# Text by image tokens as 77 extra columns of the first layer's v products

## The chip, the cores and the metric

The kernel runs on one core of a Trainium2 chip. The metric is the device time of one execution in microseconds; the median of three runs stands for a kernel. All arrays are fp32. TensorE is the matrix engine, DVE (VectorE), ACT (ScalarE) and POOL (GpSimd) are the engines for elementwise work, SP issues most of the loads.

## The reference

Two layers of cross attention from 100 queries to 722 context tokens (77 of text, 645 of image), for a batch of 8, with 640 channels in 20 heads and a context width of 1024. Both layers read the same context, with weights of their own. What bears on the change is the second layer's extra term `sem`: it needs the product of every text token with every image token of the same batch entry.

```python
# both layers: attention over the text tokens plus attention over the image tokens
text = ctx_2048[:, :77]                    # B, 77, 1024
ip   = ctx_2048[:, 77:]                    # B, 645, 1024
q = x @ Wq;  k_text = text @ Wk;  v_text = text @ Wv     # first layer: W.T
ip_k = ip @ Wk_ip;  ip_v = ip @ Wv_ip
...
# second layer only
text_probs = softmax((q @ k_text^T) * scale)             # B, 100, 77, over all 640 channels
q_sem = text_probs @ text                                # B, 100, 1024
sem   = (q_sem @ ip^T) * scale                           # B, 100, 645
fused = scores_ip + 0.5 * sem                            # the same sem for all heads
ip_probs = softmax(fused) * spatial_mask
...
out = (text_out + ip_out) @ Wout + bout + residual
```

The kernel forms `sem` as `text_probs @ (text @ ip^T)`. The inner product `text @ ip^T`, 77x645 for each batch entry and independent of the layer, is what the change makes in another place.

## The kernel before

A *unit* u is one layer of one batch entry: units 0 to 7 are the first layer, 8 to 15 the second. There are three kinds of work.

**The prologue** (some 205 us) makes the first layer's q and both layers' k and v of the text tokens, `text_k` and `text_v`/`text_v_blocks`, and in `left_v` the v rows of the last 5 of the 645 image tokens, all stored to DRAM.

**Projection of the image tokens.** Units 0 to 13 are taken in pairs of batch entries (`pair_tasks`). A pair runs over five blocks j of 128 image tokens (the last block has 133 for k, 128 for v). `load_x` brings the tokens of both entries, x with 1024 features on partitions in eight chunks. A pair and its block form a 2x2 product of halves (entry by half of the features, times half of the features by half of the channels), done with seven products in place of eight: `token_sums` makes four sums of x (DVE, POOL), `weight_sums` four sums of the weights, and `seven` runs the products named first, sixth, second, seventh, fifth, fourth, third, with PSUM tiles a to e (second adds onto a, third onto d). In `v_product` the tokens are the stationary operand and 320 weight columns stream through, four matmuls a product (line 482); in `k_product` the weights are stationary (line 490); `last_k` makes the last 128 channels of k plainly (line 461). ACT and DVE bring the results from PSUM to `vo` and `ko`, and POOL stores them to DRAM. The weights lie in quarters `wv00`, `wv01`, `wv10`, `wv11` (first digit the half of features, second the half of channels) and sums `wvt2` to `wvt4`. Unit 14 (`single_tasks`) and unit 15 (`last_tasks`) are made with plain products (`plain_product`, line 558).

The second layer's pairs also have `text_by_image`: for each of the two entries and each block, eight matmuls with 77 text columns stationary and the block's image tokens streaming (line 472, PSUM tile `psg`), an ACT copy to `gst` (line 477) and a POOL store to `g_d` (line 478). For units 14 and 15 `text_one` does the same in blocks of 256, 256 and 133 tokens. The text is loaded as `textt`.

**Attention.** Each unit has five phases p of four heads each, 80 phases in all: `scores` (in two parts), softmax on DVE and ACT, `transposes` of the probabilities (PSUM `pspt`, line 857), `values` (PSUM `pv`, line 879). For the second layer, `small_work` puts `sem_logits`, `sem_transpose` and `sem_scores` into phases 3 and 4 of the unit before; `sem_scores` multiplies the 100x77 probabilities with the loaded `g` (77x645), which `load_g` fetches from `g_d` in phase 4.

TensorE's order is written by hand. `production` spreads the projection's tasks over the phases in front of their need (`spread`, by planned times such as 2.15 for a v step), and the main loop puts them between the pieces of attention, so that TensorE has a product to do while DVE and ACT work on the softmax. The first pair is made before phase 0. PSUM has four banks for scores, two for `ps_pt` (transposes, values, small work) and two for the projection's products (`ps_pj`). The order of the other engines follows from the program and its dependences.

Of the kernel before, what the change touches and what calls it, by code (L numbers as in the profile page):

```python
# [14 lines left out]
P = 128  # L15
B = 8
# [27 lines left out]
def two_layer_xattn(  # L44
# [36 lines left out]
    g_d = [dram.tile([NT, NI], F32, tag=f"g_{b}", name=f"g_d{b}") for b in range(B)]  # L81
# [16 lines left out]

    def load_quarter(kind, rows, n, i, j):
        t = wpool.tile([P, HK, n], F32, tag=f"w{kind}{i}{j}", name=f"w{kind}{i}{j}")  # L100
        nc.sync.dma_start(t, rows[:, HK * i : HK * (i + 1), n * j : n * (j + 1)])
        W[kind, f"b{i + 1}{j + 1}"] = t

    def weight_sums(kind, n, engines):
        b11, b12, b21, b22 = (W[kind, f"b{x}"] for x in ("11", "12", "21", "22"))
        t2, t3, t4 = (wpool.tile([P, HK, n], F32, tag=f"w{kind}t{x}", name=f"w{kind}t{x}") for x in (2, 3, 4))
# [29 lines left out]
    def seven(name, product, area):  # L136

        c11, c12, c21, c22 = area
# [17 lines left out]
        def second():  # L156
            product(ps["a"], 2, True)
            nc.scalar.copy(c11, flat("a"))

# [5 lines left out]
        def fifth():  # L165
            ps["d"] = product_ps(f"{name}_d")
            product(ps["d"], 5, False)
            nc.vector.tensor_tensor(c22, flat("d"), c21, ALU.add)

        def fourth():  # L170
            ps["e"] = product_ps(f"{name}_e")
            product(ps["e"], 4, False)
            nc.vector.tensor_tensor(c21, flat("e"), c21, ALU.add)  # L173

# [5 lines left out]

    WHICH = {1: "b11", 2: "b21", 3: "b22", 4: "t4", 5: "t1", 6: "t2", 7: "t3"}
# [11 lines left out]
    with ExitStack() as es:  # L193
# [101 lines left out]
        def text_v_blocks(l):  # L295
            for r in range(2):
# [38 lines left out]

        def sums_of(kind):
            weight_sums(kind, {"v": HC, "k": 2 * P}[kind], (nc.vector, nc.gpsimd))

        with tc.manual_schedule(engines={mybir.EngineType.PE}):
# [11 lines left out]
            left_v(0)  # L351
            text_v(1)
            sums_of("v")
            load_left(1)
            text_v_blocks(1)
            sums_of("k")
            left_v(1)

# [50 lines left out]
    def load_g(u):  # L409
        t = one.tile([NT, NI], F32, tag="g", name=f"g_{u}")  # L410
        nc.sync.dma_start(t, g_d[u % B])
# [15 lines left out]
    def pair_tasks(us):  # L427
# [3 lines left out]
        if l:  # L431
            text = {}

            def load_text():
                text[0] = one.tile([P, NCC, 2 * NT], F32, tag="textt", name=f"textt_{us[0]}")
                b = us[0] % B
                nc.sync.dma_start(text[0], text_t.rearrange("k p n -> p k n")[:, :, b * NT : (b + 2) * NT])

            tasks.append((0.0, load_text))
        for j, (n0, n1) in enumerate(BLOCKS):  # L440
            n = n1 - n0
            sums, vo, ko = {}, {}, {}
# [26 lines left out]
            def text_by_image(i, j=j, n0=n0, n=n):  # L469
                ps = product_ps(f"psg_{us[i]}_{j}")  # L470
                for k in range(NCC):
                    nc.tensor.matmul(
                        ps[:NT, :n], lhsT=text[0][:, k, i * NT : (i + 1) * NT], rhs=xs[j][:, i, k, :n],
                        start=(k == 0), stop=(k == NCC - 1),
                    )
                t = one.tile([NT, NX], F32, tag="gst", name=f"gst_{us[i]}_{j}", bufs=2)
                nc.scalar.copy(t[:, :n], ps[:NT, :n])  # L477
                nc.gpsimd.dma_start(g_d[us[i] % B][:, n0 : n0 + n], t[:, :n])

            def v_product(ps, which, go_on, sums=sums):  # L480
                for k in range(HK):
                    nc.tensor.matmul(  # L482
                        ps[:, :HC], lhsT=sums[which][:, k, :P], rhs=W["v", WHICH[which]][:, k, :],
# [12 lines left out]
            def v_step(i, j=j, vo=vo, made={}, v_product=v_product):  # L496
                if i == 0:
                    o = vo[0]
                    made[j] = seven(
                        f"psv_{us[0]}_{j}", v_product, (o[:, 0, :HC], o[:, 0, HC:], o[:, 1, :HC], o[:, 1, HC:])  # L500
# [20 lines left out]
            if l:  # L521
                tasks += [(1.8, lambda i=i, f=text_by_image: f(i)) for i in range(2)]
            steps = [
                [(2.15, lambda i=i, f=v_step: f(i)) for i in range(7)],
# [583 lines left out]
```

## Time and profile before

| | |
|---|---|
| median of three runs | 2108.51 us (2107.51 to 2110.2) |
| the profiled execution | 2109.68 us |
| its span, from the first to the last instruction | 2107.6 us |
| granted TensorE clock | 1.0 |
| TensorE busy | 2084.8 us, 99% |
| DVE, ACT, POOL busy | 935.6, 861.5, 331.9 us |
| PSUM tiles of text by image (`psg`) | 30 in pairs, 6 in single units |
| attention's phases | from 381 us to the end; the second layer's units are attended from 1292 us |

In the profile a row of a group gives busy time, the mean length of one instruction in ns, and the idle time of its engine before it with what ended it. In a timeline a row gives start and length in us, engine, line, and how many instructions were merged. PE rows are matmuls, PEld rows weight loads that overlap them. One fp32 matmul of the program appears as two records, a transpose as one.

### The profile page before, as it was taken

What the parts mean: (1) busy time and instruction counts of PE and PEld (TensorE: products, weight loads), DVE (VectorE), ACT (ScalarE), POOL (GpSimd) and SP (SyncE); (2) the same over time, 40 slices, a digit from 0 to 9 for tenths busy, and PEclk for the clock granted to TensorE, in tenths of its full rate; (3) what the DMA queues carried; (4) which work ended last, traced back from release to release, by engine and by line L of the source; (5) the groups of instructions that cost most, each with busy time, mean ns of one, the idle gap of its engine ahead of it and who ended that gap; (6) DMA issues with size and microseconds to landing.
All of it is one profiled execution on the core that took longest, in us unless ns stands there. A gap on an engine that the chain in (4) does not pass through costs nothing. (4 is left out here: it accounts for less than half of the span.)

```text
span 2107.6 us, 41702 instructions
## 1 busy us (share of the span) xinstructions
PE 2084.8 (99%) x16770; PEld 1691.3 (80%) x16770; DVE 935.6 (44%) x2380; ACT 861.5 (41%) x2861; POOL 331.9 (16%) x382
## 2 busy tenths in 40 slices
PE   8999999999999999999999999999999999999999
PEld 8676888787788887877888888888888788777888
DVE  2211122455444455454544454454445445555554
ACT  1001000345444444354434444444445445566665
POOL 3313111111010111111511111011111110111110
PEclk9999999999999999999999999999999999999999
DMA  9344223224235343535434343343334254434320
GB/s 347 106 135 158 92 79 103 86 79 127 73 113 145 95 106 94 157 93 153 121 119 124 91 113 98 114 119 102 95 104 117 85 146 143 135 93 132 109 82 7
DMA packets 264623, 242.00 MB, mean 115 GB/s; under 512 B 31242, under 2 KB 233178, under 8 KB 264430
## 3 DMA queue, kind: packets, MB, share of 16 engines
q1 hardware_dynamic: 245310, 171.97, 29.3%
q0 software_dynamic: 19120, 67.37, 9.5%
q8 instruction: 132, 2.16, 0.4%
q14 instruction: 61, 0.50, 0.1%
HBM read 171.68 MB, written 67.61 MB: 114 GB/s over the span
## 5 line engine op out<-in xcount | busy, mean ns | idle before, releaser
L864 DVE COPY pt<-pspt 128x400 f32<-128x400 f32 x320 | 175.8, 568 | 188.6 <-PE pspt L857 167.1
L818 ACT ACTIVATE p<-p,st 100x512 f32<-100x512 f32 (+1 forms) x320 | 176.4, 553 | 142.2 <-DVE st L814 142.2
L818 ACT ACTIVATE p<-sc,st 100x512 f32<-100x512 f32 (+1 forms) x320 | 165.0, 529 | 138.2 <-DVE st L807 138.1
L841 ACT ACTIVATE p<-p,st 100x512 f32<-100x512 f32 x320 | 204.8, 711 | 40.5 <-DVE st L837 39.4
L857 PE MATMUL pspt<-ident,p 100*128 100x100 f32 (+1 forms) x1920 | 209.9, 250 | 5.7 <-DVE res L732 4.3
L857 PEld LDWEIGHTS pspt<-ident,p 100*128 100x128 f32 (+1 forms) x1920 | 187.5, 137 | 32.7 <-DVE res L732 7.4
L862 ACT COPY pt<-pspt 128x400 f32<-128x400 f32 (+1 forms) x160 | 78.0, 488 | 232.1 <-PE pspt L857 231.2
L482 PE MATMUL psv_a<-wv,x 128*128 128x320 f32 x560 | 164.3, 436 | 1.4 <-ACT gst L477 1.2
L482 PE MATMUL psv_d<-wv,s 128*128 128x320 f32 x560 | 164.1, 436 | 0.0
L814 DVE CUSTOM_DVE_ANT_0 p<-sc,sem 100x512 f32<-100x512 f32 (+1 forms) x320 | 138.8, 490 | 29.9 <-PE sc L801 29.8
L505 POOL DMA_DIRECT2D v_d<-vo x70 | 39.1, 558 | 666.5 <-DVE vo L173 551.8
L490 PEld LDWEIGHTS psk_a<-x,wk 128*128 128x128 f32 x1120 | 133.0, 191 | 10.1 <-DVE hs L883 3.1
L482 PEld LDWEIGHTS psv_a<-wv,x 128*128 128x128 f32 x560 | 103.1, 190 | 47.4 <-issue 7.3
L482 PEld LDWEIGHTS psv_d<-wv,s 128*128 128x128 f32 x560 | 103.9, 190 | 45.4 <-issue 3.2
L490 PE MATMUL psk_d<-s,wk 128*128 128x128 f32 (+1 forms) x1120 | 139.9, 278 | 0.0
L801 PE MATMUL sc<-k,q 32*100 32x210 f32 (+1 forms) x1280 | 138.5, 502 | 0.3 <-ACT p L826 0.3
L490 PE MATMUL psk_a<-x,wk 128*128 128x128 f32 (+1 forms) x1120 | 138.4, 276 | 0.2 <-ACT ko L149 0.2
L490 PEld LDWEIGHTS psk_d<-s,wk 128*128 128x128 f32 x1120 | 131.1, 191 | 8.2 <-issue 3.5
L807 DVE TENSOR_REDUCE st<-sc 100x4 f32<-100x2048 f32 x80 | 120.1, 1501 | 31.2 <-PE sc L801 31.2
L461 PE MATMUL psk<-x,wk 128*128 128x256 f32 (+1 forms) x560 | 131.2, 383 | 1.0 <-ACT vl L333 1.0
L517 POOL DMA_DIRECT2D k_d<-ko x70 | 58.1, 830 | 463.2 <-DVE ko L173 420.3
L461 PEld LDWEIGHTS psk<-x,wk 128*128 128x128 f32 x560 | 102.2, 188 | 24.4 <-issue 7.1
(176 smaller groups left out, 3399.7 us busy)
## 6 DMA issues: line engine op xcount, KB each, us to landing
x<-ip_t SPq DMA_DIRECT2D x56, 512.0 KB
k<-k_d SPq DMA_DIRECT2D x78, 322.5 KB
v<-v_d SPq DMA_DIRECT2D x78, 320.0 KB
v_d<-vo POOLq DMA_DIRECT2D x70, 320.0 KB, 2.5
k_d<-ko POOLq DMA_DIRECT2D x56, 320.0 KB, 6.7
o<-wo SPq DMA_DIRECT2D x40, 320.0 KB
x<-ip_t SPq DMA_DIRECT2D x16, 532.0 KB
q<-wq SPq DMA_DIRECT2D x20, 320.0 KB
```

The source lines that it names most:

```text
L461: nc.tensor.matmul(ps[:, : 2 * n], lhsT=W["k", 4][:, k, :], rhs=xs[j][:, :, k, :n], start=(k == 0), stop=(k == NCC - 1),)
L482: nc.tensor.matmul(ps[:, :HC], lhsT=sums[which][:, k, :P], rhs=W["v", WHICH[which]][:, k, :], start=(k == 0 and not go_on), stop=(k == HK ...
L490: nc.tensor.matmul(ps[:, r * n : (r + 1) * n], lhsT=W["k", WHICH[which]][:, k, r * P : (r + 1) * P], rhs=sums[which][:, k, :], start=(r == ...
L517: nc.gpsimd.dma_start(k_d[u][:, :, n0 : n0 + n], ko[0][:, h, :, :n])
L801: nc.tensor.matmul(sc[:S, i, : k1 - k0], lhsT=qs_[u][rows, c, :], rhs=ks[u, c][rows, k0:k1], start=True, stop=True)
L807: nc.vector.tensor_reduce(st[:, part, :], sc[:S, :, :n], AX.X, ALU.max, negate=True)
L814: nc.vector.tensor_tensor_reduce(out=img, in0=sc[:S, i, :n], in1=sems[u][:, k0 : k0 + n], scale=-1.0, scalar=3.0e38, op0=ALU.add, op1=ALU. ...
L818: nc.scalar.activation(p[:, i, k0 : k0 + n], img, AF.Exp, bias=st[:, part, i : i + 1], scale=sign, accum_out=st[:, 3 + part, i : i + 1],)
L841: nc.scalar.activation(p[:, i, :KA], p[:, i, :KA], AF.Copy, scale=mul[:, 0, i : i + 1])
L857: nc.tensor.transpose(ps[:rows, i * S : (i + 1) * S], pr[u, c][:, i, j * P : j * P + rows], ident[:S, :S])
L862: nc.scalar.copy(dst, src)
L864: nc.vector.tensor_copy(dst, src)
```

## The change

The products of text and image tokens are no longer made in the second layer. In the first layer, four of the seven v products of a block (first, second, fifth, fourth) get 77 more columns: behind the 320 weight columns of `wv00`, `wv10`, `wv01` and `wvt4` lie text columns of the two entries. First and second give text times image for the first entry, summed in PSUM tile a. For the second entry, fifth multiplies the sum of its token halves with the first half of the text, and fourth the second token half with the difference of the text halves (`text_sum`, on POOL). `text_of` copies the columns out (ACT for the first entry, DVE for the second) and stores both with one DMA a block. The result lies in DRAM with image tokens as rows, `g_d[pair][entry, 645, 77]`. `load_text` loads the text columns for each pair, in front of the pair before's last k products. The 5 image tokens beyond 640, which the v products do not hold, are made in the prologue by `left_text` (64 small matmuls); `load_left(1)` moves ahead, and the second half of `text_v_blocks(1)` moves behind `left_v(1)`. In the second layer, `load_g` loads the rows in phase 2 of the unit before instead of phase 4, and `sem_text` turns them into the old `g` (77x645) with six transposes on TensorE and two ACT copies in phase 3. `textt`, `text_by_image` and `text_one` go.

```diff
-    g_d = [dram.tile([NT, NI], F32, tag=f"g_{b}", name=f"g_d{b}") for b in range(B)]
+    g_d = [dram.tile([2, NI, NT], F32, tag=f"g_{g}", name=f"g_d{g}") for g in range(B // 2)]
...
+    WITH_TEXT = ("wv00", "wv01", "wv10", "wvt4")
+    wide = {}
+    def weight_tile(tag, n, name=None):
+        w = HC + NT if tag in WITH_TEXT else n
+        wide[tag] = wpool.tile([P, HK, w], F32, tag=tag, name=name or tag)
+        return wide[tag][:, :, :n]
...
+    def load_text(us):
+        for i, (tag, h) in zip((0, 0, 1, 1), (("wv00", 0), ("wv10", 1), ("wv01", 0), ("wvt4", 1))):
+            b = us[i] % B
+            nc.sync.dma_start(
+                wide[tag][:, :, HC:],
+                text_t[HK * h : HK * (h + 1)].rearrange("k p n -> p k n")[:, :, b * NT : (b + 1) * NT],
+            )
+    def text_sum():
+        t = wide["wvt4"][:, :, HC:]
+        nc.gpsimd.tensor_tensor(t, t, wide["wv01"][:, :, HC:], ALU.subtract)
...
+            beside(2, ps["a"])
...
+            beside(5, ps["d"])
...
+            beside(4, ps["e"])
...
+    TEXT_AT = {1: "wv00", 2: "wv10", 5: "wv01", 4: "wvt4"}
...
+        def left_text():
+            t = fp.tile([P, 2, NT], F32, tag="evg", name="gl", bufs=1)
+            ps = product_ps("psgl")
+            for h in range(2):
+                for k in range(NCC):
+                    for i in range(4):
+                        b = 4 * h + i
+                        nc.tensor.matmul(
+                            ps[32 * i : 32 * i + NL, h * NT : (h + 1) * NT], lhsT=left_sb[:, k, b * NL : (b + 1) * NL],
+                            rhs=text[:, k, b * NT : (b + 1) * NT],
+                            start=(h == 0 and k == 0), stop=(k == NCC - 1), skip_group_check=True,
+                        )
+            for i in range(4):
+                rows = slice(32 * i, 32 * i + NL)
+                nc.scalar.copy(t[rows], ps[rows, : 2 * NT].rearrange("p (h n) -> p h n", h=2))
+                for h in range(2):
+                    b = 4 * h + i
+                    nc.gpsimd.dma_start(g_d[b // 2][b % 2, NB * P :, :], t[rows, h])
...
             left_v(0)
+            load_left(1)
+            left_text()
             text_v(1)
             sums_of("v")
-            load_left(1)
-            text_v_blocks(1)
+            text_v_blocks(1, (0,))
             sums_of("k")
             left_v(1)
+            text_v_blocks(1, (1,))
 
     ps_sc = ctx.enter_context(tc.tile_pool(name="ps_sc", bufs=1, space=PSUM))
     ps_pt = ctx.enter_context(tc.tile_pool(name="ps_pt", bufs=2, space=PSUM))
...
-        t = one.tile([NT, NI], F32, tag="g", name=f"g_{u}")
-        nc.sync.dma_start(t, g_d[u % B])
+        b = u % B
+        t = one.tile([P, NB + 1, NT], F32, tag="gt", name=f"gt_{u}")
+        nc.sync.dma_start(t[:, :NB], g_d[b // 2][b % 2, : NB * P].rearrange("(j p) n -> p j n", p=P))
+        nc.sync.dma_start(t[:NL, NB], g_d[b // 2][b % 2, NB * P :])
...
-            def text_by_image(i, j=j, n0=n0, n=n):
-                ps = product_ps(f"psg_{us[i]}_{j}")
-                for k in range(NCC):
-                    nc.tensor.matmul(
-                        ps[:NT, :n], lhsT=text[0][:, k, i * NT : (i + 1) * NT], rhs=xs[j][:, i, k, :n],
-                        start=(k == 0), stop=(k == NCC - 1),
-                    )
-                t = one.tile([NT, NX], F32, tag="gst", name=f"gst_{us[i]}_{j}", bufs=2)
-                nc.scalar.copy(t[:, :n], ps[:NT, :n])
-                nc.gpsimd.dma_start(g_d[us[i] % B][:, n0 : n0 + n], t[:, :n])
+            def text_of(which, ps, j=j, gst=gst):
+                t = ps[:, HC : HC + NT]
+                if which == 2:
+                    gst[0] = one.tile([P, 2, NT], F32, tag="gst", name=f"gst_{us[0]}_{j}", bufs=2)
+                    nc.scalar.copy(gst[0][:, 0], t)
+                elif which == 5:
+                    nc.vector.tensor_copy(gst[0][:, 1], t)
+                else:
+                    nc.vector.tensor_tensor(gst[0][:, 1], t, gst[0][:, 1], ALU.add)
+                    nc.gpsimd.dma_start(g_d[us[0] // 2][:, j * P : (j + 1) * P, :].rearrange("i p n -> p i n"), gst[0])
...
+                w, m = W["v", WHICH[which]], HC
+                if not l and which in TEXT_AT:
+                    w, m = wide[TEXT_AT[which]], HC + NT
                 for k in range(HK):
                     nc.tensor.matmul(
-                        ps[:, :HC], lhsT=sums[which][:, k, :P], rhs=W["v", WHICH[which]][:, k, :],
+                        ps[:, :m], lhsT=sums[which][:, k, :P], rhs=w[:, k, :],
...
-            if l:
-                tasks += [(1.8, lambda i=i, f=text_by_image: f(i)) for i in range(2)]
-                [(2.15, lambda i=i, f=v_step: f(i)) for i in range(7)],
+                [(2.15 if l or i in (1, 3, 6) else 2.67, lambda i=i, f=v_step: f(i)) for i in range(7)],
...
+                if j == NB - 1 and us[0] + 2 < B:
+                    tasks.append((0.0, lambda: load_text([u + 2 for u in us])))
+                tasks += steps[1]
+                if j == NB - 1 and us[0] + 2 < B:
+                    tasks.append((0.0, text_sum))
...
-    def text_one(u, m, text, xs):
-        n0, n1 = BIG[m]
-        n = n1 - n0
-        return plain_product(
...
+    def sem_text(u, g):
+        if g == 0:
+            gs[u] = one.tile([NT, NI], F32, tag="g", name=f"g_{u}")
+        ps = ps_pt.tile([P, 512], F32, tag="pt", name=f"psm3_{u}_{g}")
+        for j in ((0, 1, 2), (3, 4, 5))[g]:
+            rows = P if j < NB else NL
+            at = (j - 3 * g) * P
+            nc.tensor.transpose(ps[:NT, at : at + rows], texts[u][:rows, j], ident[:rows, :rows])
+        n0, n1 = ((0, 3 * P), (3 * P, NI))[g]
+        nc.scalar.copy(gs[u][:, n0:n1], ps[:NT, : n1 - n0])
...
+                for i in range(2):
+                    at[i].append((0.4, lambda i=i: sem_text(w, i)))
...
+                load_g(u + 1)
...
-                if p == 4 and NU > u + 1 >= B:
-                    load_g(u + 1)
```

## The prediction

> **What bounds the kernel now.** I read the page first, then the list of waits of TensorE, then groups by form, then the timeline, because durations of pipelined matmuls overlap and only start-to-start times add up.
>
> ```profile
> PE 2084.8 (99%) x16770; PEld 1691.3 (80%) x16770; DVE 935.6 (44%) x2380; ACT 861.5 (41%) x2861; POOL 331.9 (16%) x382
> PEclk9999999999999999999999999999999999999999
> DMA  9344223224235343535434343343334254434320
> ```
>
> TensorE is busy for 99% of the span, in all slices at the full granted clock; DVE, ACT and the DMA engines have half of their time free or more.
>
> ```profile
> PE psq L224 <- DMA wq<-wq: 5.4, 1, 5.4
> PE pspt L857 <- DVE res L732: 4.3, 12, 1.3
> ...
> PE psg L472 <- ACT ko L467: 1.5, 2, 1.3
> PE psv_a L482 <- ACT gst L477: 1.2, 2, 1.1
> ```
>
> These are the longest waits and the two that touch this change. All of TensorE's waits together are some 17 us in 2107.6. So the time is the sum of what TensorE streams, and an edit is worth what it adds to that sum or takes from it. Two waits belong to the step that goes: psg holds the projection's slots of PSUM until ACT has copied.
>
> The step itself, by form, and its pace in the timeline (start, length, engine; an fp32 matmul has two records, a transpose one):
>
> ```profile
> L472 PE MATMUL psg<-x,textt 128*77 128x128 f32 x384 | 45.4, 273 | 1.4 <-ACT ko L467 1.3
> L472 PE MATMUL psg<-x,textt 128*77 128x133 f32 x96 | 11.7, 277 | 0.2 <-ACT ko L467 0.2
> L558 PE MATMUL psg<-x,textt 128*77 128x256 f32 x64 | 15.3, 382 | 0.0
> L558 PE MATMUL psg<-x,textt 128*77 128x133 f32 x32 | 4.0, 276 | 0.0
> ```
>
> ```profile
> 1616.71 3.66 PE L472 MATMUL psg<-x,textt 128*77 128x128 f32 x32
> 1620.20 0.85 PE L857 MATMUL pspt<-ident,p 100*128 100x100 f32 x8
> 1620.89 2.34 PE L482 MATMUL psv_a<-wv,x 128*128 128x320 f32 x8
> ...
> 1277.60 2.32 PE L482 MATMUL psv_c<-wvt,s 128*128 128x320 f32 x8
> 1279.75 0.85 PE L857 MATMUL pspt<-ident,p 100*128 100x100 f32 x8
> ...
> 1291.33 1.07 PE L879 MATMUL pv<-pt,v 128*32 128x100 f32 x40
> 1292.21 0.36 PE L879 MATMUL pv<-pt,vt 82*32 82x100 f32 x8
> 1292.50 1.12 PE L801 MATMUL sc<-k,q 32*100 32x512 f32 x8
> ```
>
> From the starts: 32 records of 128 columns take 3.49 us (109 ns each), 8 of 320 take 2.15 (269): 0.833 ns a column and hardly a fixed part; so 113 ns for 133 columns and 216 for 256. Eight transposes of 100 columns take 0.69 us (86 ns each). In pv, where four column groups take turns, 48 records take 1.17 us (24 ns each).
>
> **The change part by part.**
>
> *Removed on TensorE.* 24 psg tiles of 128 columns at 3.49/2 = 1.75 us are 42.0; six of 133 columns (16 records of 113 ns, 1.81 us) are 10.9; each of the two single units has two tiles of 256 columns (16 records of 216 ns, 3.46 us) and one of 1.81, 8.7 us, so 17.5. Sum 70.4 us. With them go the two waits of the list, 2.7 us: behind last_k the next users of slots are then v steps of over 2 us, as in the first layer now.
>
> *Added: 77 columns in four products.* 77 x 0.833 = 64 ns a record, 8 records a step, four steps, 20 blocks (four pairs of images, five blocks each): 0.513 x 80 = 41.0 us, all on TensorE. No row has 397 columns; above 320 I extend the slope. The weight load beside it (190 ns a row) fits under 269 ns already and gains room. Below 41 nothing is possible; above, a fixed penalty per instruction would show as a bend between 128 and 320 columns, and there is none.
>
> *Added: transposes.* sem_text makes six a unit for eight units. Five move 128 columns: 86 + 28 x 0.833 = 109 ns, 0.55 us; the sixth is tiny. The changeover to another kind of work costs 0.1 us a group (0.78 against 0.69 for eight transposes at 1279.75 and 1620.20). 0.75 a unit, 6.0 us. Here a rule speaks against the change: the Trainium skill, "TensorE: Matmul & The Clock Gate", Part 4: PE-mode transpose, gives about 275 ns for a 128x128 transpose inside a kernel and says that the full clock does not engage for it. By that, 40 transposes are 11 us and the part 13, which would bring the sum to 15 saved instead of 22. The trace disagrees: 86 ns between starts (250 ns is the length of a record, which overlaps) at a granted clock of 1.0. I take the trace and keep 13 for the upper end.
>
> *Added: left_text.* 64 matmuls, 128 records, of 5 weight columns and 77 moving ones in four column groups. The nearest row is pv at 24 ns: 3.1 us; scaled by 77/100, 2.4. I take 2.5; without overlap of groups (64 ns each) it is 8.2, kept for the upper end.
>
> *Moved in the prologue.* The second half of text_v_blocks(1) goes behind left_v(1), so wv's quarters come free some 7 us later (4.5 of left_v, 2.5 of left_text) in front of the v loads of the first pair. Cover: DVE's sum starts here when the last quarter has landed, and v is used only 17 us later:
>
> ```profile
> 203.75 1.49 DVE L109 TENSOR_TENSOR wvt<-wv,wv 128x1280 f32<-128x1280 f32 x1 [3.89 <-DMA wv<-wvi]
> 220.80 2.32 PE L482 MATMUL psv_a<-wv,x 128*128 128x320 f32 x8
> ```
>
> Between lie 12.5 us of k and 3.6 of last_k that are not moved. The quarters land 4.4 us after the last use, the two sums of DVE take 3.0, POOL's two 6.9; the text columns are queued on SP behind the quarters, so all is there at about 8 to 12 us after the last use, against 16. Nothing, with 4 us to spare; without that cover at most 5 us, once. load_left(1) moves ahead on SP, but it waits for left_v(0) either way; left_v(1) runs some 13 us earlier and still about 25 us after the issue.
>
> *Queues and other engines.* SP: 16 text loads replace five; three times they wait for the v steps of a pair's last block, and k and v loads stand behind them. SP already sits up to 30.4 us in such waits (x loads on psk_e) and no wait of TensorE on k appears. load_g becomes two loads, moves from phase 4 to 2 of a unit and has its own tile, a phase (some 25 us) ahead of its use. POOL: 36 stores of 0.54 us go, 28 come, and four text_sum of about 1 us in front of a pair's token sums; POOL is 16% busy. The new pieces in DRAM are 308 bytes; some 10000 packets come to 264623, with the DMA engines at most half busy in any slice after the prologue. ACT: 36 copies (0.26 to 0.35) go; 20 of 77 columns, 16 of 261 or 384 (0.36 to 0.48) and 4 small ones come: nearly even. DVE: 40 operations of about 0.25 us (261 ns for 128x100), 10 us in phases where it is half idle. All this is hidden as long as TensorE has other work between a tile and its copy. If it is not: a PSUM slot held 0.25 us longer in 60 places is 15 us, and 16 sem_text tiles whose ACT copy stands behind softmax work perhaps 0.5 us each, 8 us. One step of 1.8 us or more always lies between, so I put 1.4 us for all, and keep 23 for the slow rival.
>
> *Sum.* -70.4 - 2.7 + 41.0 + 6.0 + 2.5 + 1.4 = -22.2 us. The profiled execution took 2109.68 us (span 2107.6), so 2087.5 by its own time; the median of the runs is 1.2 lower: 2086.3.
>
> **The rivals.** *The gain is only partly kept (2 in 10).* In the last two units the filler of TensorE gets thin. The phase at 1972 us lasts 12.3 us with ACT busy for 8.5 and the chain scores, maximum, exponential, normalisation close behind. If the 17.5 us of the single units came back as waits for softmax, and the transposes cost what the page says, some 7 us would be left: 2093 to 2102. Against it: that phase shows no gap on TensorE.
>
> *Slower (7 in 100).* The second read of a PSUM tile holds its slot. With two slots, fifth waits for ACT's two copies of a, and first of the next product for DVE's two of e. If ACT's and DVE's queues are filled with softmax work just then, each of the 60 reads delays TensorE. It decides from (22.2 + 1.4)/60 = 0.4 us a read; at 0.6 us it would be 36 us against 23.6, so 12 us slower, 2121. For it: ACT's order is fixed and its bursts last 4 us. Against it: in the timeline of the first pair psk_c starts at 213.65, the moment at which psk_a's second round ends, so c takes the slot of b, and every slot has a step to come free in; the copies behind the seven products account for 0.2 us in the list of waits.
>
> *No change (5 in 100)*: the same at 0.4 us a read, 2104 to 2113. That the text products stay somewhere is excluded: every psg goes.
>
> **How the numbers follow.** The sum holds with 68 in 100; its own range is 2080 (a column costs as said, every changeover of the 36 psg tiles and more small waits go too) to 2092 (left_text without overlap). With the partly kept gain 88 in 100 are faster by over 0.2% (4 us, about what a measurement of this kernel can tell from no change). The range reaches from 2080 to 2098 and leaves out the slow rival, no change and the end of the partly kept case.
>
> **What would show it.** Right: no psg rows; up to 1045 us psv_a, psv_e and the first eight records of psv_d at 333 ns between starts, the other v steps and all later ones at 269; the first layer (380 to 1045 us) longer by about 31 us, the stretch from there to the end shorter by over 60; transposes to psm at about 109 ns. Wrong: waits of psv_d or psv_a on ACT or DVE gst of over 5 us in total, waits of a pspt on ACT's copy into g, waits of psv on text columns, or ACT above 70% in the last slices with gaps on TensorE.

## The result and the profile after

The kernel after takes 2102.24 us (median of six runs, 2100.84 to 2105.42), before 2108.47 (2107.51 to 2110.2): a ratio of 0.9971 (0.9959 to 0.9984), faster by 6.2 us. The forecast was 22.2 faster with a range that ended at 2098, so the direction was right, the size was not, and 16.0 us are to be found. The profiled execution took 2102.57 us.

The page of the kernel after, its span and engines:

```profile
span 2100.8 us, 40948 instructions
PE 2069.5 (99%) x16370; PEld 1635.0 (78%) x16370; DVE 941.5 (45%) x2420; ACT 863.6 (41%) x2865; POOL 332.6 (16%) x378
PEclk9999999999999999999999999999999999999999
```

The first reading is the split of the span: TensorE's busy time fell by 15.3 us, where the sum's stream terms say 20.9 (70.4 removed against 41.0, 6.0 and 2.5 added). Its idle time, the span less busy, *rose* from 22.8 to 31.3 us, where the sum has it fall by 1.3. So some 10 of the 16 us are TensorE's waits. The list of TensorE's waits after (total, times, longest) names them:

```profile
PE pspt L905 <- DVE res L779: 4.9, 15, 1.3
PE pspt L905 <- DVE pt L912: 4.3, 7, 0.7
PE pv L927 <- DVE pt L912: 3.3, 6, 1.1
PE psv_a L528 <- ACT vo L172: 2.6, 4, 1.0
PE psk_b L536 <- ACT ko L509: 1.7, 1, 1.7
```

The two waits around psg and gst, 2.7 us, are gone as forecast. The first line is 0.6 us more than before. `pspt` and `pv` on DVE's copy of transposed probabilities into `pt` have grown from 0.8 us to 7.6; the lines before were

```profile
PE pv L879 <- DVE pt L864: 0.5, 2, 0.3
PE pspt L857 <- DVE pt L864: 0.3, 1, 0.3
```

New are `psv_a` on ACT's first copy of a v step, and `psk_b` once, in the first pair.

The added work by form (busy time, mean record in ns, wait):

```profile
L528 PE MATMUL psv_a<-wv,x 128*128 128x397 f32 x320 | 114.9, 501 | 2.6 <-ACT vo L172 2.6
...
L528 PE MATMUL psv_e<-wvt,x 128*128 128x397 f32 x160 | 57.6, 502 | 0.0
L528 PE MATMUL psv_d<-wv,s 128*128 128x397 f32 x160 | 57.2, 499 | 0.0
...
L747 PE MATMUL psm<-ident,gt 128*77 128x128 f32 x40 | 7.0, 272 | 0.0
```

The 640 records of 397 columns, 40 transposes of 128 and no psg. In the timeline of the first pair (start, length):

```profile
225.63 2.84 PE L528 MATMUL psv_a<-wv,x 128*128 128x397 f32 x8
228.31 2.31 PE L528 MATMUL psv_b<-wvt,s 128*128 128x320 f32 x8
230.46 2.84 PE L528 MATMUL psv_a<-wv,x 128*128 128x397 f32 x8
```

A wide step takes 2.68 us from start to start (335 ns a record), a narrow one 2.15. By stretches of the trace, with an attention phase as the clock (us; "removal" is the experiment below that does only the removal):

| stretch | before | after | difference | removal alone less before |
|---|---|---|---|---|
| prologue, to the end of text_v | 204.7 | 207.6 | +2.9 | -0.9 |
| first pair, to phase 0 | 176.1 | 188.7 | +12.6 | 0 |
| phases 0 to 29 | 664.0 | 695.4 | +31.4 | -3.0 |
| phases 30 to 59 | 729.0 | 684.4 | -44.6 | -46.2 |
| phases 60 to 79 | 333.8 | 324.7 | -9.1 | -16.0 |

The first layer grew by what was forecast ("about 31"). From there to the end it shrank by 53.7, not by "over 60". Phases 60 to 79 are the last four units: the sum has -17.5 there for the products of the single units and +2.2 for three units of sem_text, so -15.3; they gave -9.1, and with the removal alone -16.0.

### The profile page after: what moved, and what is told of

The parts are those of the page before. It is cut to its first block, busy times and chain, and to the rows that moved or that the text cites. A ratio compares the mean times of both kernels' runs of the same rounds, so it can differ in the third digit from the quotient of the medians.

```text
span 2100.8 us, 40948 instructions
## 1 busy us (share of the span) xinstructions
PE 2069.5 (99%) x16370; PEld 1635.0 (78%) x16370; DVE 941.5 (45%) x2420; ACT 863.6 (41%) x2865; POOL 332.6 (16%) x378
## 4 chain that ended last, share of the span: by engine, by line
PE 95%; DVE 2%; ACT 1%; DMA 1%; issue 1%; SPq 0%; DVEq 0%; ACTq 0%
PE psv_a L528 8%; PE psv_d L528 8%; PE pspt L905 8%; PE psk_d L536 6%; PE sc L849 6%; PE psk_a L536 6%; PE psk L503 5%; PE pv L927 4%; PE psv L608 4%; PE psv_e L528 4%; PE psk L608 4%; PE psv_c L528 4%; PE psv_b L528 3%; PE psk_b L536 3%; PE psk_e L536 3%; PE psk_c L536 3%
## 5 line engine op out<-in xcount | busy, mean ns | idle before, releaser
L528 PE MATMUL psv_a<-wv,x 128*128 128x397 f32 (+1 forms) x560 | 185.5, 473 | 2.6 <-ACT vo L172 2.6
L528 PE MATMUL psv_d<-wv,s 128*128 128x320 f32 (+1 forms) x560 | 174.7, 455 | 0.0
```

What stands on the lines that cost most here:

```text
L528: nc.tensor.matmul(ps[:, :m], lhsT=sums[which][:, k, :P], rhs=w[:, k, :], start=(k == 0 and not go_on), stop=(k == HK - 1), skip_group_che ...
```

## The experiments

Two kernels first take the change apart, so that each half is measured on its own. Each ratio below is against the kernel before, timed beside the run, and its 95% interval is some 2 to 4 us to each side. A difference of less than 3 to 4 us between two runs is therefore, unless their ranges are well apart, not settled by their times alone; there the waits and starts in the traces are the evidence. The expectations name the runs by the short labels in brackets.

**Additions alone** (x1). The kernel after, with the second layer's text products put back, in pairs and in single units (their copies go to a tile that nobody reads, and any weight stands for the text). It says what the additions cost while the old filler of TensorE is still there.

```diff
+            def text_by_image(i, j=j, n0=n0, n=n):
+                ps = product_ps(f"psg_{us[i]}_{j}")
+                for k in range(NCC):
+                    nc.tensor.matmul(
+                        ps[:NT, :n], lhsT=W["v", "b11"][:, k % HK, :NT], rhs=xs[j][:, i, k, :n],
...
+                nc.scalar.copy(t[:, :n], ps[:NT, :n])
...
+                tasks += [(1.8, lambda i=i, f=text_by_image: f(i)) for i in range(2)]
...
```

> The changed kernel with the text products kept in the second layer as well, 30 in pairs and 6 in single units, their results unused (stationary operand: 77 weight columns; no load of text, no store). So this is the kernel before plus all that the change adds. Theory 1 (the additions stream as summed, and the gain was lost in new short waits because the removed products had stood between the pieces of attention and their copies): with the products back, the additions cost their sum, 41.7 + 6.4 + 2.2 = 50 us of TensorE time, and 2 to 5 us of waits (the prologue's, the v steps'): 2159 to 2164 us. Theory 2 (the additions themselves cost more than their streams: wide products, transposes, held slots): all of the 16 us lost belong to them, 50 + 16 = 66, 2174 us. Theory 3 (the removed products were worth less than their streams): additions cost 50 sharp, 2158.

Measured: 2165.77 us against 2108.27, ratio 1.0273 (1.0256 to 1.029): +57.5. The sum has 41.0 + 6.0 + 2.5 + 1.4 = 50.9 with its small waits. Among the waits of this kernel are `pspt` on DVE's copy, 3.0 us against 0.3 before, and `psv_a` on `vo`, 2.6; both come back below.

**Removal alone** (x2). The kernel before, without the text products; the stores into `g_d` take rows of x, so `sem` comes from other numbers and these DMAs stay; the loads of the text go. The step costs the plan nothing now, so the other filler moves up.

```diff
-                ps = product_ps(f"psg_{us[i]}_{j}")
-                for k in range(NCC):
-                    nc.tensor.matmul(
-                        ps[:NT, :n], lhsT=text[0][:, k, i * NT : (i + 1) * NT], rhs=xs[j][:, i, k, :n],
...
-                nc.gpsimd.dma_start(g_d[us[i] % B][:, n0 : n0 + n], t[:, :n])
+                nc.gpsimd.dma_start(g_d[us[i] % B][:, n0 : n0 + n], xs[j][:NT, i, 0, :n])
...
-                tasks += [(1.8, lambda i=i, f=text_by_image: f(i)) for i in range(2)]
+                tasks += [(0.0, lambda i=i, f=text_by_image: f(i)) for i in range(2)]
...
```

> The kernel before without the text products of the second layer, nothing in their place: their matmuls, ACT copies and text loads are left out, rows of x are stored to the same DRAM tiles instead, so sem is made from other numbers. The stream that goes is 70.2 us, and 2.7 us of waits with it. Theory 1: the removal alone already brings less, because TensorE is left without filler in the last two units: 5 to 10 us come back as waits, most of them from 1774 us on; 2041 to 2045 us. Theory 2: the removal brings its whole 73 us, 2035. Theory 3: it brings 16 less, 57, 2051, without waits to show for it.

Measured: 2043.02 us, ratio 0.9693 (0.9678 to 0.9707): -65.3, where the sum has -73.1. The halves add to -7.8, the whole gives -6.2, a difference of 1.6 us, which is within the intervals.

The removal's page and list of waits show what is missing:

```profile
span 2041.5 us, 40473 instructions
PE 2015.0 (99%) x16194; PEld 1624.8 (80%) x16194; DVE 934.1 (46%) x2380; ACT 852.8 (42%) x2825; POOL 331.9 (16%) x382
```

```profile
PE pspt L831 <- DVE res L706: 6.2, 16, 1.3
...
PE pv L853 <- DVE pt L838: 4.3, 6, 2.4
PE pspt L831 <- DVE pt L838: 1.7, 3, 0.7
```

Busy fell by 69.8 us, so the 70.4 of the stream is right within a per cent. But idle rose from 22.8 to 26.5, where two waits of 2.7 went: 6.4 us of other waits came in, of the 7.8 that are missing. The longest, in the timeline of this kernel:

```profile
1240.75 0.85 PE L831 MATMUL pspt<-ident,p 100*128 100x100 f32 x8
1241.44 1.92 PE L452 MATMUL psk<-x,wk 128*128 128x256 f32 x8
...
1243.39 1.78 DVE L668 TENSOR_SCALAR tp<-tp,sst 100x77 f32<-100x77 f32 x1
1243.82 1.29 POOL L187 TENSOR_TENSOR s<-x,s 128x512 f32<-128x512 f32 x1
...
1245.10 0.56 DVE L838 COPY pt<-pspt 128x400 f32<-128x400 f32 x1
...
1245.71 1.07 PE L853 MATMUL pv<-pt,v 128*32 128x100 f32 x40 [2.36 <-DVE pt L838]
```

DVE comes to its copy late, behind a softmax step of the small work, and `pv` stands for 2.36 us. The same place before, where a psg tile stands directly in front of `pv`:

```profile
1260.27 0.85 PE L857 MATMUL pspt<-ident,p 100*128 100x100 f32 x8
1260.96 3.65 PE L461 MATMUL psk<-x,wk 128*128 128x256 f32 x16
1264.44 1.91 PE L472 MATMUL psg<-x,textt 128*77 128x128 f32 x16
1266.28 1.06 PE L879 MATMUL pv<-pt,v 128*32 128x100 f32 x40
```

From the transposes to `pv` TensorE has 6.0 us of its own to do here, and in the removal 2.6: the psg tile is gone, and half of `psk` has moved in front of the transposes. The size of the wait has a second cause. DVE's step takes about 0.25 us in six of its eight places and 1.78 here, and it ends 0.06 us after POOL's sum of tokens. In the kernels before, after and with the removal alone, another short softmax step on DVE (the product with the mask, median 0.23 us) took over 0.5 us 14 times; each time it ended 0.02 to 0.04 us after an operation of POOL. So some 1.5 of the 2.36 us go with POOL's work, and the 6.0 us of before would have covered them. In the kernel after, `pv` waits 1.01 us at this place.

**Without the columns** (x3). The kernel after, with 320 columns in every v product (the text columns are read from inside the 320, so all copies, sums and stores stay).

```diff
-                t = ps[:, HC : HC + NT]
+                t = ps[:, :NT]
...
-                    w, m = wide[TEXT_AT[which]], HC + NT
+                    w, m = wide[TEXT_AT[which]], HC
```

> The changed kernel, but the four wide v products stream 320 columns as before; the copies and stores of the 77 columns stay and read the first 77 columns of the same tiles, so the text product is left out. Order of TensorE as in the changed kernel. Theories 1 and 3: 640 records at 65 ns less, 41.7 us: 2060.5 us, with the waits of the changed kernel still there. Theory 2 with a penalty on wide products: more than 46 us less, under 2056.

Measured: 2057.24 us (0.9759, 0.9744 to 0.9773), so the columns cost 45.0 us against 41.0. By all starts in the first pair the wide record takes 334.2 ns and the narrow one 269.1, so the stream is 65.1 x 640 = 41.7. The rest is waits: psk_b happens to stand for 0.3 us here instead of 1.7 (it varies, see the prologue below), and psv_a's 2.6 us vanish from the list; 41.7, 1.4 and 2.6 are 45.7, which is 0.7 more than was found. Two timelines show why. After:

```profile
460.79 2.94 PE L528 MATMUL psv_a<-wv,x 128*128 128x397 f32 x8
460.93 2.29 DVE L855 TENSOR_REDUCE st<-sc 100x4 f32<-100x2048 f32 x1 [0.78 <-PE sc L849]
...
463.26 0.69 ACT L866 ACTIVATE p<-sc,st 100x512 f32<-100x512 f32 x1 [1.45 <-DVE st L855]
...
465.92 0.43 ACT L172 COPY vo<-psv_a 128x320 f32<-128x320 f32 x1
466.41 2.94 PE L528 MATMUL psv_a<-wv,x 128*128 128x397 f32 x8 [0.52 <-ACT vo L172]
```

The same place without the columns:

```profile
443.47 2.42 PE L528 MATMUL psv_a<-wv,x 128*128 128x320 f32 x8
...
445.93 0.42 ACT L172 COPY vo<-psv_a 128x320 f32<-128x320 f32 x1 [1.45 <-PE psv_a L528]
446.25 0.69 ACT L866 ACTIVATE p<-sc,st 100x512 f32<-100x512 f32 x1
```

Both engines get their input at nearly the same moment: the v product starts with the maximum of the scores on DVE (2.29 us). The narrow product (2.26 us to the next) comes in first and its copy goes ahead of the exponentials; the wide one (2.78) comes in second, and in ACT's order the copy is behind four exponentials, 2.66 us. `second` adds onto the same PSUM tile and must wait. Four such places (1.01 and three times 0.52) make 2.6 us.

**Without the transposes** (x4). sem_text makes no transposes and no copies; `g` is filled by one DMA with the same bytes in another shape, so that `sem` comes from other numbers, and the places that the plan keeps for sem_text stay.

```diff
-        for j in ((0, 1, 2), (3, 4, 5))[g]:
...
-            nc.tensor.transpose(ps[:NT, at : at + rows], texts[u][:rows, j], ident[:rows, :rows])
...
-        nc.scalar.copy(gs[u][:, n0:n1], ps[:NT, : n1 - n0])
+            nc.sync.dma_start(gs[u], g_d[b // 2][b % 2].rearrange("i n -> (i n)").rearrange("(n i) -> n i", i=NI))
...
```

> The changed kernel without the transposes of sem_text and their ACT copies: g is loaded by one DMA that reads the same bytes in another shape, so sem is made from other numbers. The planned places of sem_text stay, empty. By the stream alone 6.4 us less, 2095.8. Theory 1 adds the waits that they cause (the transposes of probabilities behind each take 0.25 to 0.3 us longer for want of a PSUM slot, and 2.8 us in front of two pv): 10 to 13 us less, 2089 to 2092. Theory 2 in the form of the skill page's 275 ns a transpose: 13 us or more, with no change of the rows behind them. Theory 3: 6.

Measured: 2094.46 us (0.9934, 0.9919 to 0.9949): the transposes cost 7.8 us, against 6.0 by the trace and 13 by the rule. In the starts of the kernel after, 32 of the 128-row transposes take 109 ns or little more, as forecast; the eight directly in front of a tiny one take 201, which makes 128 in the mean (5.1 us), and the eight tiny ones of 5x5 157 ns each (1.3). That is 6.4 us of stream; the 1.4 us above it are within the interval. The list of waits is unchanged to the tenth at `pspt` and `pv`, so those waits are not the transposes' doing.

**The prologue's order put back** (x5).

```diff
-            text_v_blocks(1, (0,))
+            text_v_blocks(1)
             sums_of("k")
             left_v(1)
-            text_v_blocks(1, (1,))
```

> The changed kernel with the prologue's order as before: text_v_blocks(1) whole, then left_v(1) last (left_text stays). Theory 1, for the part at the start: the wait of 1.7 us of psk_b for ACT's copy into ko is the store of the last text v block, which frees the memory under ko; it goes, about 1 us of wait on left_v comes as before: 1 to 2 us less than the changed kernel, 2101. If the wait comes from the loads of wv or the text columns instead, it stays: no difference, with the same row of 1.7 us.

Measured: 2099.26 us, ratio 0.9961 (0.9948 to 0.9973): 3.0 less than after by the medians, 2.1 by the ratios, whose intervals overlap. The wait of psk_b is gone from the list, and with it the question is what held ACT's copy. The timeline of the kernel after around that wait:

```profile
208.01 0.55 POOL L336 DMA_DIRECT2D vt_d<-vt  x1 [1.85 <-DMA wv<-text_t]
...
212.88 1.49 DVE L131 TENSOR_TENSOR wvt<-wv,wv 128x1280 f32<-128x1280 f32 x1 [5.42 <-DMA wv<-wvi]
...
214.38 0.37 ACT L509 COPY ko<-psk 128x256 f32<-128x256 f32 x1 [15.60 <-DVE wvt L131]
...
214.81 1.38 PE L536 MATMUL psk_b<-s,wkt 128*128 128x128 f32 x10 [1.72 <-ACT ko L509]
```

ACT's copy of the plain k product, long since ready in PSUM, begins at 214.38, and with it psk_b gets its slot. The profile puts it down to DVE's sum, which ends at the same moment. In another kernel with this order (the copy on DVE, below) the two come apart:

```profile
212.05 1.49 DVE L131 TENSOR_TENSOR wvt<-wv,wv 128x1280 f32<-128x1280 f32 x1 [5.10 <-DMA wv<-wvi]
213.50 0.37 ACT L510 COPY ko<-psk 128x256 f32<-128x256 f32 x1 [15.23 <-DMA vt_d<-vt]
```

ACT begins before DVE's sum ends, and the row names the last store of the text's v rows. In the seven executions with the new order, this one and the kernel after among them, ACT begins 0.68 us after that store has landed; in four of them DVE's sum runs for some 0.05 us more or longer. The store, issued at 208.01 in the kernel after, lands 5.7 us later. So it was not the loads of `wv`, which the forecast had weighed, but a store that the new order makes late, as the expectation of this run had it. That `ko` waits because it lies in memory that the stored tile held is that expectation's reason; no run tests it. The wait varies with the landing, from 0.3 to 1.9 us between the kernels with this order.

**Another PSUM slot for sem_text** (x6). The rival of slots, put to the test: sem_text takes a slot of the products instead of one that the probabilities' transposes use. If ps_pt were short, time is won.

```diff
-        ps = ps_pt.tile([P, 512], F32, tag="pt", name=f"psm3_{u}_{g}")
+        ps = product_ps(f"psm3_{u}_{g}")
```

> The changed kernel with sem_text's two PSUM tiles taken from the projection's slots instead of those of the transposes. If the slot that sem_text holds until ACT has copied costs anything beyond the 6.4 us of its own stream (x4 left 7.8 us behind in all), up to 1.5 us go: 2100.5 to 2102. If its place behind the softmax work of ACT then delays the products instead, 1 to 3 us more: 2103 to 2105.

Measured: 2115.6 us, ratio 1.0035 (1.0022 to 1.0047), slower than both kernels and 13.4 us above after. In its list of waits the old ones at `pspt` and `pv` are unchanged to the tenth; among the new ones are:

```profile
PE psv L608 <- ACT vo L610: 3.0, 2, 1.6
...
PE psv_a L528 <- ACT ko L509: 2.3, 2, 1.8
PE psm L747 <- DVE ko L177: 2.2, 3, 1.0
```

So sem_text's use of the ps_pt slots was not what made `pspt` and `pv` wait. A third user of the two product slots turns ACT's place in its queue into TensorE's wait, 1 to 1.8 us at a time.

**Finer filler** (x8). With the text products gone, small steps of attention stand next to each other. This run cuts the plain products of the last units into pieces half as long, so that more of these places can get one.

```diff
-        parts = 2 if time > 2.5 else 1
+        parts = 4 if time > 2.5 else 2
```

> The changed kernel with plain products (units 14 and 15) cut into four pieces, or two where there was one, so that there are twice as many pieces of filler of half the size. No work is added or taken. Theory 1 (what the removal gave back is lost where two pieces of small work and transposes follow each other with no filler between, since there are too few pieces): most of the six waits of 0.67 us and the three of 0.32 from 1786 us on go, and eight transposes behind psm take 0.7 us again instead of 1.55: 4 to 6 us less, 2096 to 2098. If the loss in the last units is ACT or DVE at their limit, cutting changes nothing: 2101 to 2103.

Measured: 2106.29 us (13 runs), ratio 0.9993 (0.9985 to 1.0001): 4 us slower than after, a miss. The places are filled, but with pieces of 0.9 us: the wait of `pspt` on DVE's copy grew from 4.3 to 6.2 us, those on ACT's copies came in, and TensorE's busy time rose from 2069.5 to 2072.8 us. Two of the waits:

```profile
PE pspt L905 <- DVE pt L912: 6.2, 10, 0.7
...
PE psv L608 <- ACT v L610: 1.1, 1, 1.1
```

There is no more work than before to share out, either: phases 50 to 59 take 213.8 us against 216.6 after, and from phase 75 to the end, where it is missing, 93.8 against 89.2.

**The first copy of a wide step on DVE** (x9). It takes the copy out of ACT's queue behind the exponentials, in steps of v only.

```diff
-            nc.scalar.copy(c11, flat("a"))
+            (nc.vector.tensor_copy if wide_v else nc.scalar.copy)(c11, flat("a"))
```

> The changed kernel with the copy of the first v product of the first layer's blocks made by DVE instead of ACT. Theory 1 for the first layer: the longer first product lets the copy slip behind four exponentials in ACT's order, and second, which adds onto the same PSUM tile, waits (four waits, 2.6 us). On DVE the copy stands behind the row maximum alone: those waits go, 2 to 3 us less, 2099 to 2100. If the wait is for the 397 columns themselves or for TensorE's drain, it stays.

Measured: 2096.68 us, ratio 0.9948 (0.9935 to 0.9962), 5.5 us less than after by the medians. The wait of psv_a has gone from the list, and phases 0 to 9 take 217.7 us against 221.4, 3.7 less, of which the waits are 2.6. The execution is already 0.9 ahead at psk_b of the first pair, in front of the first v step, where the edit has changed nothing; the last us is the distance of the profiled executions from their medians.

**Both repairs together** (c1): the prologue's order and the copy on DVE.

```diff
-            text_v_blocks(1, (0,))
+            text_v_blocks(1)
...
-            nc.scalar.copy(c11, flat("a"))
+            (nc.vector.tensor_copy if wide_v else nc.scalar.copy)(c11, flat("a"))
```

> The changed kernel with both mends that each gained alone: the prologue's order as before, and the first product's copy on DVE in the first layer. Their waits lie in different stretches (start of the first pair, phases 1 to 7), so by theory 1 they add: 3.0 + 5.5 = 8.5 at most by the medians, 4.5 to 5.5 by the waits alone: 2094 to 2097.5 us. If one only moved the other's wait, 2097 or more.

Measured: 2095.57 us, ratio 0.994 (0.9928 to 0.9952): 6.7 us less than after, against 8.5 if the two medians added; the difference is within the intervals.

**A longer look ahead** (c2) for filler, on top of these. In the main loop `apart` takes one more product when the next piece of attention would follow without one; it may take it up to 0.4 us ahead of its plan. Here 0.8, and sem_text one place later.

```diff
-                    at[i].append((0.4, lambda i=i: sem_text(w, i)))
+                    at[i + 1].append((0.4, lambda i=i: sem_text(w, i)))
...
-                apart(n + b + 0.4)
+                apart(n + b + 0.8)
...
-            apart(n + b + 0.4)
+            apart(n + b + 0.8)
```

> c1, and in the main loop a longer look ahead (apart takes a filler task that is planned up to 0.8 of a phase later, instead of 0.4, so that small work and transposes are parted), with sem_text one place later in its phase. No work added or taken. In TensorE's order small work stands directly before transposes 15 times instead of 35. Theory 1 (eight transposes take 1.55 us behind psm and 1.2 behind pso instead of 0.69): 20 places at 0.4 to 0.8 us, 5 to 10 us less than c1: 2085 to 2091. As x8 has shown, filler that is taken here is missing elsewhere: if that holds in the last units only, 2 to 4 us less than c1; if everywhere, no gain, 2094 to 2097.

Measured: 2093.2 us (2092.58 to 2093.72), ratio 0.9928 (0.9915 to 0.994), the fastest kernel here: 2.4 below both repairs alone, 9.0 below after. Of its waits, `pv` on DVE fell from 3.3 us to 1.4 and `pspt` on DVE's residual from 4.9 to 2.2, and a new one of 2.2 came:

```profile
PE pspt L905 <- ACT tp L727: 2.2, 1, 2.2
PE pspt L905 <- DVE res L779: 2.2, 6, 1.3
```

**sem_text without time in the plan** (c3), with both repairs: its place costs the plan nothing, so that products are not put off for it.

```diff
-                    at[i].append((0.4, lambda i=i: sem_text(w, i)))
+                    at[2 * i].append((0.0, lambda i=i: sem_text(w, i)))
```

> c1 with sem_text given no planned time and its two pieces in the first and third place of the phase. It tests whether the 0.8 us that the plan reserves for it in phase 3 push filler out of phases 3 and 4 (six waits of 0.67 us in the last units in the kernel with the reserved places but no transposes, two in the kernel with the removal alone). If so, two to four of these waits go, 1.5 to 3 us less than c1: 2092 to 2094; if not, the same as c1.

Measured: 2096.92 us (2096.35 to 2099.25), ratio 0.995 (0.9937 to 0.9964): no gain over both repairs alone, a miss. `pv` on DVE fell to 1.1 us, but `pspt` on the residual rose to 6.2 and a wait of 2.2 on ACT's `tp` came. Five of the six stops of 0.67 us that the kernel after has in its last units (see below) are still there. The planned times of sem_text do not explain the loss.

**The longer look in the kernel before** (b1). Whether the last gain belongs to the change:

```diff
-                apart(n + b + 0.4)
+                apart(n + b + 0.8)
...
-            apart(n + b + 0.4)
+            apart(n + b + 0.8)
```

> The kernel before with the longer look ahead alone. In its order small work stands directly before transposes 9 times instead of 23. If parting them is worth 0.4 us a place whatever the filler is, 5 to 6 us less, 2102 to 2104, and c2's gain over c1 is no merit of the change; if the filler is then missing elsewhere, 2107 to 2110.

Measured: 2100.97 us, ratio 0.9966 (0.9954 to 0.9979), 7.4 us faster than before and a little faster than the kernel after. `pspt` on the residual falls from 4.3 us to 2.0. So the look ahead is a gain of its own, larger here than behind the change. Between kernels that both have it, the change with its repairs is worth 2100.97 - 2093.2 = 7.8 us. The copy on DVE was not tried in the kernel before, whose list has no wait of `psv_a` on `vo`.

## Why the prediction was right and wrong

It failed in one main step and some smaller ones; forecast and measured, in us:

| step of the sum | forecast | measured | missing |
|---|---|---|---|
| removed products and waits | -73.1 | -65.3 (removal alone) | 7.8 |
| 77 columns | 41.0 | 45.0 (without columns) | 4.0 |
| transposes | 6.0 | 7.8 (without transposes) | 1.8 |
| left_text, small waits, prologue | 3.9 | 4.7 (additions less the two above) | 0.8 |
| the halves do not quite add | 0 | 1.6 | 1.6 |
| sum | -22.2 | -6.2 | 16.0 |

*"Removed on TensorE" was mis-sized by what was left out of it.* The stream term held: 70.4 against 69.8 of busy time, and the two waits went too. The step that failed is the sentence "All this is hidden as long as TensorE has other work between a tile and its copy". The prediction used it for the copies that are added. It applies as much to the copies that stay: the 36 psg tiles, of 1.75 us or more, were part of that other work, and with them gone 6.4 us of waits came in. They are on DVE's copies and sums out of PSUM: `pspt` and `pv` on `pt` from 0.8 us to 6.0, `pspt` on the residual from 4.3 to 6.2. The place in front of `pv`, above, shows a psg tile before and a wait of 2.36 us without it. A removal that leaves the order of all other work as it was has not been run, so what the tiles themselves covered is not parted from what moved when the plan closed up.

In the last units the loss is not the removal's alone. After:

```profile
1851.81 0.71 PE L756 MATMUL psm<-g,tpt 77*100 77x323 f32 x2
1852.36 0.51 PE L905 MATMUL pspt<-ident,p 100*128 100x100 f32 x4
1853.53 0.55 PE L905 MATMUL pspt<-ident,p 100*82 100x100 f32 x4 [0.67 <-DVE pt L912]
```

The transposes follow `psm` directly: the first four go to one ps_pt slot, the next four find the other still held and stop for 0.67 us, and a set that takes 0.69 us behind a product takes 1.55. The same place with the additions alone, where the psg tiles are back:

```profile
1902.34 1.95 PE L620 MATMUL psg<-x,wv 128*77 128x256 f32 x8
1904.13 0.71 PE L778 MATMUL psm<-g,tpt 77*100 77x323 f32 x2
...
1905.85 0.54 PE L927 MATMUL pspt<-ident,p 100*82 100x100 f32 x4 [0.67 <-DVE pt L934]
```

The stop is there too. Stops of 0.67 us in the last units: none before, two with the removal alone, four with the additions alone, six after, and six without the transposes. So the additions changed TensorE's order there as well, which the sum has nowhere; what in them does it stays open, since taking out the transposes leaves all six, and taking out their planned time five.

*The rivals.* The partly kept gain was the nearest, at 2 in 10, but placed too narrowly: of what is missing in the removal only 1.5 us lie in the single units (16.0 against 17.5), the rest where second-layer pairs are made. The waits are for copies and sums out of PSUM that come late in DVE's queue. Its sum was wrong too: 22.2 less 17.5 and 7 is 2.3 us slower, not 7 faster, so that its upper end of 2102 lies next to the result is luck. The slower rival, slots held by the second read of a PSUM tile, is visible nowhere in the kernel after: no wait of TensorE names `gst`. A slot does cost much when a copy in ACT's queue holds it (the run with sem_text in a product slot, +13.4), so the mechanism is real, and the change's own reads do not set it off.

*"77 columns".* 64 ns a record were forecast, 65.1 measured; the extended slope holds to 397 columns. What failed is that a longer product was taken to cost only its length. It also changed which of two pieces of work reaches ACT first, 2.6 us; the run that moves this copy to DVE shows no such wait. Another 1.4 us of the comparison is psk_b's wait, which varies.

*"Transposes".* The trace was the better guide, as chosen. The Trainium skill, "TensorE: Matmul & The Clock Gate", Part 4: PE-mode transpose, gives about 275 ns; here, in fp32, 272 is the length of a record, and 109 ns is what most of them add, at a granted clock of 1.0. The tiny sixth transpose, called nothing, takes 157 ns between starts and lengthens the one in front of it to 201; 6.4 us of stream for 6.0.

*"Moved in the prologue: nothing, with 4 us to spare".* Wrong by 2 to 3 us. The cover was counted for the loads of v. The term left out is the last store of the text's v rows, which the move makes later: ACT's first copy into `ko` starts 0.68 us after it has landed, and the k steps stand behind that copy.

*left_text* took 2.2 us between its start and the next work (160.75 to 163.00), as said (2.5). SP, POOL and DMA: no wait of TensorE names text columns or a load of `g`.

Of the last column only the 7.8 stands clear of its interval (about 3 us). For the 4.0 the starts and waits above speak; the 1.8, 0.8 and 1.6 are not told from noise. Of the 7.8, 6.4 is in the new waits of the removal; the remaining 1.4 stay without a place.

## What to carry to other kernels

On an engine that is busy for 99% of the span, an edit's worth is not its stream alone: independent work that is removed was also the cover of other engines' copies (2.36 us of wait at one `pv` without it), so look at what will follow what in that engine's order, and take off the part of each copy that shows. A step made longer is checked for the queue that it now enters second. Before a loss is repaired in the changed kernel, the repair is run in the old one too: the longer look ahead gained more there.

## What was not expected of the hardware

- Eight transposes of 100 columns take 0.69 us behind a long product, and 1.55 us in six of the eight places directly behind `psm`: 0.67 is the wait for one DVE copy of 0.56 us.
- A 5x5 transpose takes 157 ns from start to start, and a 128x128 one 109, or 201 when the 5x5 one follows it.
- A DVE step of 0.25 us took 1.78 us while POOL added tokens, and ended 0.06 us after POOL did.
- Cutting products of the same total length into halves cost 4 us in all.
- Packets under 512 bytes rose by some 11500 (the new pieces in DRAM are 308 bytes), all packets by some 7900, and no wait of TensorE on a DMA grew by more than 0.2 us.
